# Depthwise convolution accumulated in PSUM four rows at a time, with a frequency stage on single PSUM banks

## The chip, the cores and the metric

One core of one Trainium2 chip runs the whole program. The metric is the device time in microseconds, taken as the median of the runs. An execution's engines are named as in the profile: PE is TensorE's matmuls and PEld its weight loads, DVE is VectorE, ACT is ScalarE, POOL is GpSimd, SP issues the DMAs. SBUF is the on-chip working memory; PSUM is the small memory that matmuls write, eight banks of 512 float32 per partition.

## The reference

Eight images of 128 x 128 pixels and 64 channels, float32, go through two layers.

```python
# layer 0: criss-cross attention
Q, K, V = x @ w_q + b_q, x @ w_k + b_k, x @ w_v + b_v
att = softmax(concat(energies along H (diagonal masked), energies along W))
x = gamma * (att_H applied to V + att_W applied to V) + x
# layer 1: frequency mixing, then a convolutional MLP
h  = layernorm(x) @ w_te + b_te                       # 64 -> 128 channels
F  = fft2(h)                                          # over H and W
fc = gelu(concat(real(F), imag(F)) @ w_fc + b_fc)     # 256 -> 256
sp = real(ifft2(fc[..., :128] + 1j * fc[..., 128:]))
x1 = x + sp @ w_tp + b_tp                             # 128 -> 64
h2 = layernorm(x1) @ w_fe + b_fe                      # 64 -> 128
d  = gelu(depthwise 3x3 convolution of h2 + b_dw)     # 128 channels, SAME padding
out = x1 + d @ w_fp + b_fp                            # 128 -> 64
```

## The kernel before

The program has two parts, one after the other. `attention` runs all eight images in an order written out by hand, and writes its result to DRAM. `mixer` does layer 1; its instructions are ordered by a scheduler, which takes the order of the program as priority and places an instruction when its inputs and buffers are free by its own reckoning. Every engine then works through its own queue in that fixed order. The change is inside `mixer`.

**The frequency stage**, `fourier(b)`, yields after every piece of work, so that other work can be put between. It has three stages. In the W stage, 64 matmuls (L558, tile `aps`) apply the Fourier transform along W, eight channels into one PSUM tile of two banks; ScalarE copies each tile into `at` (L559). In the K stage there are 17 groups of up to four frequencies. A group's transform along H goes through `fps` (L571, L577, L580) and is copied to `f` (L582). One group later, four matmuls of 128 x 512 (`fcps`, L595) apply the 256 x 256 weights: for each half of the output channels, one matmul with `wplus` and one with `wminus`, into the two banks of one PSUM tile. One gelu on ScalarE (L601) empties both banks into `gl`, and GpSimd adds or subtracts the two (L602). One group later still, `gps` (L622; L612 to L616 in the last group, which holds the mean) applies the projection to 64 channels, and ScalarE copies it to `gt` (L625). In the I stage, `inverse_h` transforms back along H (`yps`, L649 to L657), and `inverse_w` transforms back along W (`dps`, L663, two matmuls of 512 into a tile of two banks) while VectorE adds the result to the residual (L669).

**The convolution**, `mlp(b)`, works through an image in 16 chunks of eight rows, with the 128 hidden channels on the partitions. `statistics` (L688) computes the layernorm's deviations on VectorE; `normed` (L694, GpSimd), `transposed` (L703, TensorE) and `expand` (L724, TensorE; L729, ScalarE) make a chunk's hidden rows `h2`. `taps` then accumulates the nine taps of the 3x3 filter for eight rows (1024 elements per partition) in the SBUF tile `acc`: tap 0 on ScalarE with the bias (L746), taps 1 to 8 on VectorE, one `scalar_tensor_tensor` each (L748), which reads `h2` and `acc` and writes `acc`. `gelu` runs on ScalarE in place (L755). `shrink` (L765 on GpSimd, L770 on TensorE) computes the output projection of eight rows, and `store` (L774) adds the residual on VectorE and issues the DMA to DRAM.

**What sets the order.** The driver at the end of `mixer` runs `fourier(b)` and, between its pieces, `mlp(b-1)`: a step of the frequency stage has a weight (`W_STEP`, `K_STEP`, `I_STEP`), and the convolution's 89 pieces are dealt out in proportion. So the first image's frequency stage runs without a convolution, and the last image's convolution without a frequency stage. `load_norm(b+1)` (L542) is put into the I stage.

**PSUM.** The eight banks of `mixer` belong to three pools: `ps_f` (tag `fc`: `aps`, `fcps`, `dps`), two tiles of two banks; `ps_m` (tag `mm`: `fps`, `gps`, `yps`), two of one bank; `ps_c` (tag `mc`: `tpn`, `hp`, `op`), two of one bank. All eight are taken.

Of the kernel before, what the change touches and what calls it, by code (L numbers as in the profile page):

```python
# [21 lines left out]
F32 = mybir.dt.float32  # L22
BF16 = mybir.dt.bfloat16
AF = mybir.ActivationFunctionType
ALU = mybir.AluOpType
# [12 lines left out]
W_STEP, K_STEP, I_STEP = 2.0, 7.0, 5.0  # L38
# [396 lines left out]
def mixer(tc, nc, x2, scale1, tbl, prm, out):  # L435
# [3 lines left out]
    with ExitStack() as ctx:  # L439
# [3 lines left out]
        ps_c = ctx.enter_context(tc.tile_pool(name="m_psc", bufs=2, space=PSUM))  # L443

# [106 lines left out]
        def fourier(b):  # L551
# [3 lines left out]
            for c0 in range(0, C, 8):  # L555
                aps = ps_f.tile([P, 8, P], F32, tag="fc", name="aps")
                for c in range(8):
                    nc.tensor.matmul(aps[:, c, :], lhsT=xn[:, c0 + c, :], rhs=fwd, start=True, stop=True)  # L558
                nc.scalar.copy(at[:, :, c0 : c0 + 8], aps.rearrange("p c k -> p k c"))  # L559
                yield W_STEP  # L560
            gt = big.tile([P, C, 2, 64], F32, tag="big", name="gt")
            pend_fc, pend_tp = None, None
            for g in groups + [None, None]:
# [21 lines left out]
                if pend_fc is not None:  # L585
                    gg, f = pend_fc
                    n = len(gg) * P
                    fv = f.rearrange("p k h -> p (k h)")[:, 0:n]
                    gs = []
                    for half in range(2):  # L590
                        ps = ps_f.tile([P, 2, 512], F32, tag="fc", name="fcps")
                        cols = slice(half * HID, half * HID + HID)
                        for sgn, w in enumerate((wplus, wminus)):
                            mean = gg[0] == 0
                            nc.tensor.matmul(ps[:, sgn, 0:n], lhsT=w[:, cols], rhs=fv, start=True, stop=not mean)  # L595
                            if mean:
                                nc.tensor.matmul(
                                    ps[:, sgn, 0:1], lhsT=dc[:, cols], rhs=ident[0:1, 0:1], start=False, stop=True
                                )
                        gl = p2.tile([P, 2, 512], F32, tag="gl%d" % half, name="gl")  # L600
                        nc.scalar.activation(gl[:, :, 0:n], ps[:, :, 0:n], AF.Gelu, bias=bfc[:, half : half + 1])  # L601
                        nc.gpsimd.tensor_tensor(  # L602
                            gl[:, 0, 0:n], gl[:, 0, 0:n], gl[:, 1, 0:n], ALU.add if half == 0 else ALU.subtract
                        )
                        gs.append(gl)
                    tp_next = (gg, gs)
# [53 lines left out]
        def inverse_w(xs, c0, ys):  # L660
            dps = ps_f.tile([P, 8, P], F32, tag="fc", name="dps")
            for g in range(2):
                nc.tensor.matmul(  # L663
                    dps[:, 4 * g : 4 * g + 4, :].rearrange("p c h -> p (c h)"), lhsT=idw,
                    rhs=ys[:, 4 * g : 4 * g + 4, :].rearrange("p c h -> p (c h)"), start=True, stop=True,
                )
            for s in range(2):
                xv = xs[s][:, :, c0 : c0 + 8]
                nc.vector.tensor_tensor(xv, dps[:, :, 64 * s : 64 * s + 64].rearrange("p c h -> p h c"), xv, ALU.add)  # L669
# [8 lines left out]
        def mlp(b):  # L678
# [4 lines left out]
            xts, h2s, accs = {}, {}, {}  # L683
# [50 lines left out]
            def span(k):  # L734

                return (1 if k == 0 else 0), (CH + 1 if k == n_ch - 1 else CH)

            def taps(k, lo, hi):
                i0, i1 = span(k)
                if lo == 0:  # L740
                    accs[k] = p2.tile([P, CH + 1, P], F32, tag="acc", name="acc")
                av = accs[k][:, 0 : i1 - i0, :]
                for t in range(lo, hi):
                    src = h2s[k][:, i0 + t // 3 : i1 + t // 3, t % 3 : t % 3 + P]
                    if t == 0:
                        nc.scalar.activation(av, src, AF.Identity, bias=bdw, scale=wdw[:, 0:1])  # L746
                    else:
                        nc.vector.scalar_tensor_tensor(  # L748
                            out=av, in0=src, scalar=wdw[:, t : t + 1], in1=av, op0=ALU.mult, op1=ALU.add
                        )  # L750

            def gelu(k):
                i0, i1 = span(k)
                av = accs[k][:, 0 : i1 - i0, :]
                nc.scalar.activation(av, av, AF.Gelu)  # L755

            def shrink(k, a):
# [11 lines left out]
                for i in range(n):  # L769
                    nc.tensor.matmul(op[:, i, :], lhsT=accs[k][:, a + i, :], rhs=wfp, start=True, stop=True)  # L770
# [15 lines left out]
            taps(0, 0, 1)  # L786
            for k in range(n_ch):
                if k > 0:
                    gelu(k - 1)
# [4 lines left out]
                taps(k, 1, 3)  # L794
                yield
                held = shrink(k - 1, 0) if k > 0 else None
                taps(k, 3, 5)
# [3 lines left out]
                taps(k, 5, 6)  # L801
# [5 lines left out]
                taps(k, 6, 8)  # L807
                yield
                if k + 1 < n_ch:
                    taps(k + 1, 0, 1)  # L810
                taps(k, 8, 9)
                yield
            gelu(n_ch - 1)
# [7 lines left out]
        work = W_STEP * 8 + K_STEP * (len(groups) + 2) + I_STEP * 9  # L821
# [65 lines left out]
```

## Time and profile before

| | |
|---|---|
| time, median of 3 | 3831.16 us (3825.0 to 3836.74) |
| span of the profiled execution | 3833.7 us |
| PE busy | 3370.7 us (88%) |
| DVE busy | 2676.3 us (70%) |
| ACT busy | 1741.7 us (45%) |
| POOL busy | 1607.0 us (42%) |
| attention (0 to 1363 us): PE / DVE busy | 1200.6 / 761.3 us |
| mixer (1363 to 3834 us, 2471 us): PE / DVE / ACT / POOL busy | 2170.1 / 1915.0 / 1161.0 / 1127.0 us |
| DMA | 242.94 MB, mean 63 GB/s |

How to read it. A row of the slices has one digit per fortieth of the span (96 us): the tenths of that time in which the engine was busy. A row of a window has its start and end, its length, then the busy time (and number of instructions) of PE, PEld, DVE, ACT and POOL, the granted share of TensorE's clock, the DMA share and GB/s. A row of a group has the line, the engine, the operation, what it writes and reads by the program's tile names and shapes, how often; then its busy time in all and the mean of one in ns; then the idle time of that engine just before it and what ended most of it. A row of the timeline has a start, a duration, and the merged instructions. A row of the waits says which engine and line waited for which, for how long in all, how often, and the longest. A float32 matmul is executed as two passes, so the trace counts it twice. The ends of matmuls are modelled, so a busy TensorE need not be one at its full rate.

### The profile page before, as it was taken

What the parts mean: (1) busy time and instruction counts of PE and PEld (TensorE: products, weight loads), DVE (VectorE), ACT (ScalarE), POOL (GpSimd) and SP (SyncE); (2) the same over time, 40 slices, a digit from 0 to 9 for tenths busy, and PEclk for the clock granted to TensorE, in tenths of its full rate; (3) what the DMA queues carried; (4) which work ended last, traced back from release to release, by engine and by line L of the source; (5) the groups of instructions that cost most, each with busy time, mean ns of one, the idle gap of its engine ahead of it and who ended that gap; (6) DMA issues with size and microseconds to landing.
All of it is one profiled execution on the core that took longest, in us unless ns stands there. A gap on an engine that the chain in (4) does not pass through costs nothing.

```text
span 3833.7 us, 79138 instructions
## 1 busy us (share of the span) xinstructions
PE 3370.7 (88%) x33046; PEld 2387.3 (62%) x33046; DVE 2676.3 (70%) x4432; ACT 1741.7 (45%) x2341; POOL 1607.0 (42%) x1347
## 2 busy tenths in 40 slices
PE   7989989899998679998998998998998998999454
PEld 4666666666666457666665666666665665666333
DVE  3556565664665500788888987888988988978867
ACT  3544535435353233453553553553553554554222
POOL 0333243332433534356356356356356356253111
PEclk7989889999897889998998998998998998999555
DMA  4534434354342511012112112112112112100000
GB/s 101 128 94 121 109 98 124 93 129 108 91 119 69 170 44 45 6 39 58 37 39 58 37 39 58 37 39 58 37 39 58 37 39 53 37 17 17 12 19 20
DMA packets 505190, 242.94 MB, mean 63 GB/s; under 512 B 417026, under 2 KB 486018, under 8 KB 502786
## 3 DMA queue, kind: packets, MB, share of 16 engines
q1 hardware_dynamic: 504834, 237.90, 23.1%
q8 instruction: 260, 4.26, 0.5%
q14 instruction: 96, 0.79, 0.1%
HBM read 169.13 MB, written 67.63 MB: 62 GB/s over the span
## 4 chain that ended last, share of the span: by engine, by line
PE 52%; DVE 26%; issue 8%; POOL 6%; ACT 4%; DMA 2%; SPq 1%; DVEq 0%; POOLq 0%; ACTq 0%
DVE acc L748 18%; PE e L202 6%; PE op L770 5%; PE fcps L595 5%; PE hp L724 4%; PE zp L265 3%; PE yps L655 3%; PE dps L663 3%; PE yps L649 3%; PE sp L289 3%; PE pq L183 3%; PE zp L278 3%; POOL xn L542 2%; PE gps L622 2%; DVE negH L211 2%
## 5 line engine op out<-in xcount | busy, mean ns | idle before, releaser
L748 DVE SCALAR_TENSOR_TENSOR acc<-h,wdw,acc 128x1024 f32<-128x1024 f32 (+2 forms) x1024 | 1612.1, 1594 | 151.5 <-ACT acc L746 131.2
L602 POOL TENSOR_TENSOR gl<-gl 128x512 f32<-128x512 f32 (+2 forms) x272 | 487.1, 1796 | 454.0 <-ACT gl L601 453.9
L770 PE MATMUL op<-wfp,acc 128*128 128x64 f32 x2048 | 292.0, 304 | 163.7 <-ACT acc L755 162.8
L770 PEld LDWEIGHTS op<-wfp,acc 128*128 128x128 f32 x2048 | 278.2, 218 | 187.9 <-ACT acc L755 180.0
L601 ACT ACTIVATE gl<-fcps,bfc 128x1024 f32<-128x1024 f32 (+2 forms) x272 | 292.5, 1077 | 190.7 <-PE fcps L595 180.9
L765 POOL TENSOR_TENSOR ot<-x,bfp 128x512 f32<-128x512 f32 (+1 forms) x144 | 226.2, 1576 | 358.9 <-DMA out_dram<-ot 321.8
L243 ACT ACTIVATE att<-e 128x1024 f32<-128x1024 f32 x256 | 248.3, 1022 | 242.9 <-PE e L202 242.8
L339 POOL TENSOR_TENSOR yo<-yo,xb 128x512 f32<-128x512 f32 x128 | 161.0, 1280 | 430.4 <-issue 296.3
L245 POOL TENSOR_SCALAR_AFFINE_SELECT att<-att 128x1024 f32<-128x1024 f32 x128 | 136.8, 1093 | 419.6 <-ACT att L243 419.6
L729 ACT ACTIVATE h<-hp,bfe 128x512 f32<-128x512 f32 x256 | 171.4, 688 | 291.3 <-PE hp L724 291.1
L595 PE MATMUL fcps<-f,wplus 128*128 128x512 f32 (+2 forms) x544 | 293.7, 622 | 0.0
L622 PEld LDWEIGHTS gps<-wtp,gl 128*128 128x128 f32 x2016 | 246.0, 193 | 57.7 <-issue 55.2
L595 PE MATMUL fcps<-f,wminus 128*128 128x512 f32 (+2 forms) x544 | 275.9, 589 | 0.0
L669 DVE TENSOR_TENSOR x<-dps,x 128x512 f32<-128x512 f32 x128 | 86.2, 683 | 265.2 <-PE dps L663 265.2
L542 POOL TENSOR_TENSOR xn<-xl,scale 128x512 f32<-128x512 f32 x128 | 238.4, 1873 | 57.1 <-DMA xl<-x 56.9
L724 PE MATMUL hp<-xtn,wfe 64*128 64x512 f32 x512 | 243.6, 739 | 21.1 <-DVE ot L774 19.8
L755 ACT ACTIVATE acc<-acc 128x1024 f32<-128x1024 f32 (+2 forms) x128 | 135.4, 1058 | 258.6 <-DVE acc L748 258.6
L202 PE MATMUL e<-qkH 8*128 8x128 f32 (+1 forms) x4096 | 199.7, 316 | 54.4 <-DVE negH L211 50.3
L694 POOL TENSOR_TENSOR xc<-x,scale 128x512 f32<-128x512 f32 x128 | 189.1, 1482 | 129.2 <-PE tpn L703 88.2
L622 PE MATMUL gps<-wtp,gl 128*128 128x64 f32 x2016 | 241.1, 273 | 0.9 <-POOL gl L602 0.9
L202 PEld LDWEIGHTS e<-qkH 8*128 8x128 f32 (+1 forms) x4096 | 164.3, 212 | 122.1 <-DVE negH L211 60.0
L202 PEld LDWEIGHTS e<-qkW 8*128 8x128 f32 (+1 forms) x4096 | 140.6, 194 | 126.4 <-DVE negW L211 36.0
(138 smaller groups left out, 6389.1 us busy)
## 6 DMA issues: line engine op xcount, KB each, us to landing
xl<-in_x_dram SPq DMA_DIRECT2D x256, 128.0 KB
xh<-in_x_dram SPq DMA_DIRECT2D x64, 512.0 KB
xw<-in_x_dram SPq DMA_DIRECT2D x256, 128.0 KB
x<-yo SPq DMA_DIRECT2D x256, 128.0 KB
xl<-x SPq DMA_DIRECT2D x128, 256.0 KB
x<-x SPq DMA_DIRECT2D x16, 2048.0 KB
out_dram<-ot SPq DMA_DIRECT2D x120, 256.0 KB
qkH<-joint SPq DMA_DIRECT2D x256, 2.0 KB
```

The costliest lines, as they stand in the source:

```text
L202: nc.tensor.matmul(es[q // 2][:, q % 2, i, :], lhsT=qk[part, lhs, 4 * (r % 2) + i, :], rhs=qk[part, rhs, 4 * (r % 2) + i, :], start=True, ...
L243: nc.scalar.activation(att, e.rearrange("p q i w -> p (q i) w"), AF.Exp)
L542: nc.gpsimd.tensor_tensor(xn[:, :, h : h + NORM_ROWS], xl.rearrange("p h c -> p c h"), scale1[:, b, h : h + NORM_ROWS].unsqueeze(1).to_bro ...
L595: nc.tensor.matmul(ps[:, sgn, 0:n], lhsT=w[:, cols], rhs=fv, start=True, stop=not mean)
L601: nc.scalar.activation(gl[:, :, 0:n], ps[:, :, 0:n], AF.Gelu, bias=bfc[:, half : half + 1])
L602: nc.gpsimd.tensor_tensor(gl[:, 0, 0:n], gl[:, 0, 0:n], gl[:, 1, 0:n], ALU.add if half == 0 else ALU.subtract)
L622: nc.tensor.matmul(gps[:, j, t, :], lhsT=src[:, 0, j * P : j * P + P], rhs=wtp, start=True, stop=True)
L694: nc.gpsimd.tensor_tensor(xc, rows, scale[:, k * CH : k * CH + CH].unsqueeze(2).to_broadcast([P, CH, C]), ALU.mult)
L724: nc.tensor.matmul(hps[s].rearrange("p j w -> p (j w)"), lhsT=wfe[half, :], rhs=xt[half, :, :].rearrange("p j w -> p (j w)"), start=True, ...
L748: nc.vector.scalar_tensor_tensor(out=av, in0=src, scalar=wdw[:, t : t + 1], in1=av, op0=ALU.mult, op1=ALU.add)
L765: nc.gpsimd.tensor_tensor(ot[:, o : o + m, :], rows, bfp.unsqueeze(1).to_broadcast([P, m, C]), ALU.add)
L770: nc.tensor.matmul(op[:, i, :], lhsT=accs[k][:, a + i, :], rhs=wfp, start=True, stop=True)
```

## The change

Four things go together.

1. The convolution's accumulator moves from SBUF to a new PSUM pool, `ps_a`, of two single banks. A bank holds four rows of 128 pixels, so a chunk's eight rows become two half-chunks (the first chunk has 3 + 4 rows, the last 4 + 4 + 1). Each half has its own chain of nine taps and its own gelu, which reads PSUM and writes a new SBUF tile `gd`, from which the output matmuls read. A tap on VectorE then has one input in SBUF (`h2`) and one in PSUM, and writes PSUM.
2. To free two banks, `ps_f` holds two tiles of one bank in place of two tiles of two. The W stage works in fours of channels instead of eights.
3. In the K stage each of the four matmuls of a group has a bank and a gelu of its own: 512 elements per gelu in place of 1024.
4. In the I stage each of the two matmuls of `inverse_w` has its own bank and its own two adds, of 256 elements in place of 512.

The order in which `mlp` writes out its pieces is drawn up anew for half-chunks, and the W stage's step weight is halved as its steps are doubled. The arithmetic is the same.

```diff
--- before.py
+++ after.py
@@ -35,7 +35,7 @@
 CH = 8
 NORM_ROWS = 8
 
-W_STEP, K_STEP, I_STEP = 2.0, 7.0, 5.0
+W_STEP, K_STEP, I_STEP = 1.0, 7.0, 5.0
 PIECES = 5
 LEAD = 6
 
@@ -441,6 +441,7 @@
         ps_f = ctx.enter_context(tc.tile_pool(name="m_psf", bufs=2, space=PSUM))
         ps_m = ctx.enter_context(tc.tile_pool(name="m_psm", bufs=2, space=PSUM))
         ps_c = ctx.enter_context(tc.tile_pool(name="m_psc", bufs=2, space=PSUM))
+        ps_a = ctx.enter_context(tc.tile_pool(name="m_psa", bufs=2, space=PSUM))
 
         ident = const.tile([P, P], F32, tag="ident", name="m_ident")
         make_identity(nc, ident)
@@ -552,11 +553,11 @@
             im = images[b]
             xn = im["xn"]
             at = big.tile([P, P, C], F32, tag="big", name="at")
-            for c0 in range(0, C, 8):
-                aps = ps_f.tile([P, 8, P], F32, tag="fc", name="aps")
-                for c in range(8):
+            for c0 in range(0, C, 4):
+                aps = ps_f.tile([P, 4, P], F32, tag="fc", name="aps")
+                for c in range(4):
                     nc.tensor.matmul(aps[:, c, :], lhsT=xn[:, c0 + c, :], rhs=fwd, start=True, stop=True)
-                nc.scalar.copy(at[:, :, c0 : c0 + 8], aps.rearrange("p c k -> p k c"))
+                nc.scalar.copy(at[:, :, c0 : c0 + 4], aps.rearrange("p c k -> p k c"))
                 yield W_STEP
             gt = big.tile([P, C, 2, 64], F32, tag="big", name="gt")
             pend_fc, pend_tp = None, None
@@ -588,17 +589,17 @@
                     fv = f.rearrange("p k h -> p (k h)")[:, 0:n]
                     gs = []
                     for half in range(2):
-                        ps = ps_f.tile([P, 2, 512], F32, tag="fc", name="fcps")
+                        gl = p2.tile([P, 2, 512], F32, tag="gl%d" % half, name="gl")
                         cols = slice(half * HID, half * HID + HID)
                         for sgn, w in enumerate((wplus, wminus)):
+                            ps = ps_f.tile([P, 512], F32, tag="fc", name="fcps")
                             mean = gg[0] == 0
-                            nc.tensor.matmul(ps[:, sgn, 0:n], lhsT=w[:, cols], rhs=fv, start=True, stop=not mean)
+                            nc.tensor.matmul(ps[:, 0:n], lhsT=w[:, cols], rhs=fv, start=True, stop=not mean)
                             if mean:
                                 nc.tensor.matmul(
-                                    ps[:, sgn, 0:1], lhsT=dc[:, cols], rhs=ident[0:1, 0:1], start=False, stop=True
+                                    ps[:, 0:1], lhsT=dc[:, cols], rhs=ident[0:1, 0:1], start=False, stop=True
                                 )
-                        gl = p2.tile([P, 2, 512], F32, tag="gl%d" % half, name="gl")
-                        nc.scalar.activation(gl[:, :, 0:n], ps[:, :, 0:n], AF.Gelu, bias=bfc[:, half : half + 1])
+                            nc.scalar.activation(gl[:, sgn, 0:n], ps[:, 0:n], AF.Gelu, bias=bfc[:, half : half + 1])
                         nc.gpsimd.tensor_tensor(
                             gl[:, 0, 0:n], gl[:, 0, 0:n], gl[:, 1, 0:n], ALU.add if half == 0 else ALU.subtract
                         )
@@ -658,15 +659,15 @@
             return ys
 
         def inverse_w(xs, c0, ys):
-            dps = ps_f.tile([P, 8, P], F32, tag="fc", name="dps")
             for g in range(2):
+                dps = ps_f.tile([P, 4, P], F32, tag="fc", name="dps")
                 nc.tensor.matmul(
-                    dps[:, 4 * g : 4 * g + 4, :].rearrange("p c h -> p (c h)"), lhsT=idw,
+                    dps.rearrange("p c h -> p (c h)"), lhsT=idw,
                     rhs=ys[:, 4 * g : 4 * g + 4, :].rearrange("p c h -> p (c h)"), start=True, stop=True,
                 )
-            for s in range(2):
-                xv = xs[s][:, :, c0 : c0 + 8]
-                nc.vector.tensor_tensor(xv, dps[:, :, 64 * s : 64 * s + 64].rearrange("p c h -> p h c"), xv, ALU.add)
+                for s in range(2):
+                    xv = xs[s][:, :, c0 + 4 * g : c0 + 4 * g + 4]
+                    nc.vector.tensor_tensor(xv, dps[:, :, 64 * s : 64 * s + 64].rearrange("p c h -> p h c"), xv, ALU.add)
 
         def lines(xs, lo, hi):
 
@@ -680,7 +681,7 @@
             xs = images.pop(b)["x1"]
             n_ch = P // CH
             scale = p2.tile([P, P], F32, tag="scale2", name="scale2")
-            xts, h2s, accs = {}, {}, {}
+            xts, h2s, accs, gls = {}, {}, {}, {}
 
             def statistics(s):
                 stats = p2.tile([P, 64, 6], F32, tag="stats", name="stats", bufs=1)
@@ -735,11 +736,16 @@
 
                 return (1 if k == 0 else 0), (CH + 1 if k == n_ch - 1 else CH)
 
-            def taps(k, lo, hi):
+            def part(k, u):
+
                 i0, i1 = span(k)
+                return max(i0, 4 * u), min(i1, 4 * u + 4)
+
+            def taps(k, u, lo, hi):
+                i0, i1 = part(k, u)
                 if lo == 0:
-                    accs[k] = p2.tile([P, CH + 1, P], F32, tag="acc", name="acc")
-                av = accs[k][:, 0 : i1 - i0, :]
+                    accs[k, u] = ps_a.tile([P, 4, P], F32, tag="acc", name="acc")
+                av = accs[k, u][:, 0 : i1 - i0, :]
                 for t in range(lo, hi):
                     src = h2s[k][:, i0 + t // 3 : i1 + t // 3, t % 3 : t % 3 + P]
                     if t == 0:
@@ -749,10 +755,11 @@
                             out=av, in0=src, scalar=wdw[:, t : t + 1], in1=av, op0=ALU.mult, op1=ALU.add
                         )
 
-            def gelu(k):
-                i0, i1 = span(k)
-                av = accs[k][:, 0 : i1 - i0, :]
-                nc.scalar.activation(av, av, AF.Gelu)
+            def gelu(k, u):
+                i0, i1 = part(k, u)
+                if u == 0:
+                    gls[k] = p2.tile([P, CH + 1, P], F32, tag="gd", name="gd")
+                nc.scalar.activation(gls[k][:, i0 : i1, :], accs.pop((k, u))[:, 0 : i1 - i0, :], AF.Gelu)
 
             def shrink(k, a):
 
@@ -767,7 +774,7 @@
                     )
                 op = ps_c.tile([P, CH, C], F32, tag="mc", name="op")
                 for i in range(n):
-                    nc.tensor.matmul(op[:, i, :], lhsT=accs[k][:, a + i, :], rhs=wfp, start=True, stop=True)
+                    nc.tensor.matmul(op[:, i, :], lhsT=gls[k][:, i0 + a + i, :], rhs=wfp, start=True, stop=True)
                 return r0, n, ot, op
 
             def store(r0, n, ot, op):
@@ -783,34 +790,39 @@
             yield
             expand(0)
             yield
-            taps(0, 0, 1)
+            taps(0, 0, 0, 1)
             for k in range(n_ch):
                 if k > 0:
-                    gelu(k - 1)
+                    gelu(k - 1, 1)
+                taps(k, 1, 0, 1)
                 if k + 1 < n_ch:
                     transposed(k + 1)
                 if k == 4:
                     statistics(1)
-                taps(k, 1, 3)
+                taps(k, 0, 1, 4)
                 yield
                 held = shrink(k - 1, 0) if k > 0 else None
-                taps(k, 3, 5)
+                taps(k, 0, 4, 8)
                 yield
                 if held:
                     store(*held)
-                taps(k, 5, 6)
+                taps(k, 0, 8, 9)
+                gelu(k, 0)
+                taps(k, 1, 1, 3)
                 yield
                 if k + 1 < n_ch:
                     expand(k + 1)
                 if k + 2 < n_ch:
                     normed(k + 2)
-                taps(k, 6, 8)
+                taps(k, 1, 3, 6)
                 yield
                 if k + 1 < n_ch:
-                    taps(k + 1, 0, 1)
-                taps(k, 8, 9)
+                    taps(k + 1, 0, 0, 1)
+                taps(k, 1, 6, 9)
                 yield
-            gelu(n_ch - 1)
+            gelu(n_ch - 1, 1)
+            taps(n_ch - 1, 2, 0, 9)
+            gelu(n_ch - 1, 2)
             for a in (0, CH):
                 store(*shrink(n_ch - 1, a))
             yield
@@ -818,7 +830,7 @@
 
 
         pieces = LEAD + 3 + PIECES * (P // CH)
-        work = W_STEP * 8 + K_STEP * (len(groups) + 2) + I_STEP * 9
+        work = W_STEP * 16 + K_STEP * (len(groups) + 2) + I_STEP * 9
         for _ in load_norm(0):
             pass
         for b in range(NB + 1):
```

## The prediction

> **What bounds the kernel now.** I read first the page's slices of the span, then windows cut at the stages, then the groups by shape, the waits of one period, and last the timeline around single instructions.
>
> ```profile
> PE   7989989899998679998998998998998998999454
> DVE  3556565664665500788888987888988988978867
> 1363.00:1552.00 189.00, 186.63 (x1336) 137.59 (x1337) 9.02 (x14) 74.67 (x93) 65.93 (x51) 0.98 0.09 26
> 2128.00:2417.00 289.00, 266.09 (x1721) 189.10 (x1720) 245.63 (x299) 145.05 (x193) 151.77 (x118) 0.94 0.16 44
> 3587.00:3834.00 247.00, 115.34 (x376) 80.78 (x376) 175.59 (x150) 70.87 (x95) 36.34 (x58) 0.50 0.08 17
> ```
>
> Attention (0 to 1363 us) is not touched. From there the kernel has three regimes. At 1363 to 1552 the first image's frequency stage runs alone: TensorE (first busy figure) 187 of 189 us, so it is TensorE's. Then come six periods of about 290 us (one is 2128 to 2417), each the frequency stage of image b beside the convolution of image b-1, and a last such stretch of 272 us (3288 to 3560). From 3587 the last convolution runs alone, 247 us, with TensorE at half its clock (0.50).
>
> A period has two nearly full engines, TensorE 266 us and VectorE 246 of 289. TensorE's floor comes from the trace: adding the gaps over 150 ns between matmul starts beyond the streaming time leaves 186 us of work in the lone stage and 259 in a period, so the convolution adds 73, and about 31 us of a period are TensorE waiting. Two thirds of it is ahead of convolution matmuls (L770, L724, L703) and of the mean's matmuls (L612, L613).
>
> ```profile
> L748 DVE SCALAR_TENSOR_TENSOR acc<-h,wdw,acc 128x1024 f32<-128x1024 f32 x896 | 1442.9, 1630 | 129.9 <-ACT acc L746 110.1
> L602 POOL TENSOR_TENSOR gl<-gl 128x512 f32<-128x512 f32 x240 | 435.6, 1820 | 444.7 <-ACT gl L601 444.5
> 2104.68 0.68 DVE L669 TENSOR_TENSOR x<-dps,x 128x512 f32<-128x512 f32 x1
> 2105.28 1.27 DVE L748 SCALAR_TENSOR_TENSOR acc<-h,wdw,acc 128x1024 f32<-128x1024 f32 x1
> 2106.47 0.68 DVE L669 TENSOR_TENSOR x<-dps,x 128x512 f32<-128x512 f32 x1
> ...
> 2206.84 2.59 DVE L748 SCALAR_TENSOR_TENSOR acc<-h,wdw,acc 128x1024 f32<-128x1024 f32 x2
> ...
> 2208.15 3.61 DVE L748 SCALAR_TENSOR_TENSOR acc<-h,wdw,acc 128x1024 f32<-128x1024 f32 x2
> ...
> 2212.97 2.30 POOL L602 TENSOR_TENSOR gl<-gl 128x512 f32<-128x512 f32 x1 [2.30 <-ACT gl L601]
> 2215.32 2.17 POOL L602 TENSOR_TENSOR gl<-gl 128x512 f32<-128x512 f32 x1
> ```
>
> The taps (L748) are two thirds of VectorE's work in a period. One tap of 1024 alone lasts 1.27 us and gives way to the next independent instruction after 1.19 (2105.28 to 2106.47). A tap directly behind the tap it depends on starts 1.31 later (two in 2.59). Beside a GpSimd tensor_tensor it lasts 2.2 to 2.3 (the pair in 3.61), and the GpSimd instruction takes 2.2 to 2.3 instead of about 1.27. Of the 1024 taps 552 overlap one and average 1.86 us; the other 472 average 1.28. That is 552 x 0.58 = 320 us of VectorE time lost to the overlap, and about as much of GpSimd's.
>
> ```profile
> ACT acc L755 <- DVE acc L748: 18.9, 8, 7.2
> DVE acc L748 <- ACT acc L746: 17.6, 6, 4.1
> DVE ot L774 <- PE op L770: 16.5, 5, 7.4
> PEld op L770 <- ACT acc L755: 7.3, 7, 5.1
> ```
>
> These waits of one period (1837 to 2128: total, times, longest) go round one ring: taps, gelu (L755), output matmul (L770), store add (L774), and the first tap on ScalarE (L746).
>
> **What the Trainium skill says.** "SBUF — State Buffer", section Who interferes with whom: a VectorE instruction with two SBUF inputs contends with a GpSimd instruction that reads SBUF, and one with at most one SBUF input does not. The trace agrees on the first half (1.28 against 2.2); L669, with one input in PSUM, is never stretched (mean 683 ns). "Perfetto Trace Analysis", section Optimizing Scalar/DVE Operations: VectorE's overhead per instruction is about 60 ns on SBUF and about 125 on PSUM. The trace shows less for a PSUM input: L669 of 512 elements gives way after 0.60, 0.07 over its 0.53 of elements; a PSUM output is shown nowhere. "TensorE: Matmul & The Clock Gate", section Part 1, says that an idle TensorE window of some 3.4 us halves the clock: the lone convolution does run at 0.50.
>
> **The change, part by part.**
>
> *Taps into PSUM.* 1024 taps become 2112: 1984 of 512 elements, 64 of 384, 64 of 128. From 1024 to 1152 elements an undisturbed tap grows from 1274 to 1407 ns, 1.04 ns per element, so 512 elements stream in 0.53. The slot adds 0.13 (1.19 - 1.07) to an independent tap and 0.25 (1.31 - 1.07) to one behind its own predecessor. The compiled order puts only 317 taps directly behind their predecessor (440 of 1024 before): the two half-chunks alternate. So 317 x 0.78 + 1795 x 0.66 = 1432, less 34 for the small ones: 1398 us. Bounds: L669's overhead (0.60) gives 1271; 65 ns more each, the page's difference of PSUM and SBUF, gives 1535. I take the middle: the trace's PSUM inputs are no dearer, PSUM outputs are unknown. Now: 1024 x 1.594 = 1632, less 0.08 each by which the next starts early, 1552. VectorE saves 154 us (17 to 281), 19 per image.
>
> *GpSimd* no longer meets the taps: L602 falls from 1.8 to about 1.27. It is not full (152 of 289), but its sum stands between gelu and the next matmuls (L612, L622), some 5 us of TensorE's waits.
>
> *Inverse-W adds.* 128 of 0.60 become 256 of 0.34: +9 us in all.
>
> *ScalarE.* The gelu of the frequency stage: 272 x 1.077 becomes 544 x 0.684 (the row of 512): +80. First taps: 0.81 for 512 (1242 ns at 1024, 0.85 per element less): 205 for 159, +45. Convolution gelu: 264 of 0.63 for 128 of 1.06, +28. Copies of `at`: +10. Sum 163 us, 20 per period: ScalarE goes from 145 to 165 of 289, room enough by itself.
>
> *Single banks.* A matmul of 128x512 takes 0.86 (both passes). Bank one is free 0.86 + 0.1 + 0.68 = 1.65 after the start, and the third matmul wants it at 1.72: it just fits if ScalarE comes at once. Where ScalarE is inside another instruction, TensorE waits and everything behind it in its queue with it: two such places in each of 17 groups, ScalarE about two thirds busy there, half an instruction (0.35): up to 8 us per period. The order places output and expand matmuls in between, so I take 4. In the lone first stage ScalarE is idle: +2 in all. `at` in fours: four matmuls take 0.86, the copy 0.58, hidden. The finer step count moves nothing by itself.
>
> *Period.* 290 less half of TensorE's 31 us of waiting, as the ring's VectorE link shortens by 18 of 246 and loses its jitter, plus 4: 279. Seven stretches: -77.
>
> *Last convolution.* Now two chunks of eight rows take 30.8 us, 15.4 each: L774 waits 6.67 and 1.07 in the queue, with taps stuck behind it. After: 16 taps, 13 x 0.66 + 3 x 0.78 = 10.9, the store add 0.60, and 0.7 of wait (gelu 0.63, half the output matmuls at half clock 1.7, handovers 0.35, less three taps placed ahead, 2.0): 12.2. Sixteen chunks: -51; I take -40 for waits not seen.
>
> Sum: -77 + 2 - 40 = -115: 3831 - 115 = 3716.
>
> **The rivals.** (a) *TensorE's floor is reached*: periods of 265, tail -50: 3831 - 7 x 25 - 50 = 3606. For it: TensorE has 259 us of work. Against: the ring and the in-order queues stay, and ScalarE gets more to do. (b) *The gain is eaten by ScalarE*: TensorE waits 8 or more for banks while a gelu waits for taps; periods stay at 290, only the tail gains 35: 3796. For it: ScalarE's queue stops 19 us per period for taps already. (c) *Slower*: taps cost the upper price, 0.72 and 0.85, so VectorE gains nothing that counts, and with 20 us more on ScalarE and single banks the periods grow by 10; tail -20: 3831 + 70 - 20 = 3881. For it: no instruction of the trace writes PSUM from VectorE. Against: PSUM inputs come cheap, and the overlap with GpSimd ends in any case.
>
> **How the numbers follow.** Forecast 0.60 (3716), (a) 0.12, (b) 0.15, (c) 0.13. The range reaches from halfway to (a), 3630, to just past no change, 3838: it holds the forecast and (b) and leaves out most of (a) and (c). Faster by over 0.3% (below 3820) takes the forecast, (a) and most of (b): 0.83; within 0.3% 0.05; slower 0.12.
>
> **What would show it.** Right: taps of 512 lasting 0.70 to 0.80 wherever GpSimd works; L602 near 1.27; a period of 270 to 285 with TensorE's granted clock nearer 1; two chunks of the tail in 24 to 26 us. Wrong: taps over 0.85 (the PSUM price), or matmuls of `fcps` waiting for `gl` over 10 us per period (the banks).

## The result and the profile after

The changed kernel takes 3777.27 us (median of 4 runs, 3772.59 to 3780.67), the kernel before beside it 3828.08 us: ratio 0.987, 95% interval 0.9837 to 0.9904. That is 51 us gained where 115 were forecast. The direction is right and the time lies in the range, but less than half of the gain came.

Cut at the same stages as in the prediction (starts from the first `aps` matmul of each image, the tail from the last `dps` matmul), the two profiled executions give, in us:

| stage | before | after | forecast of the change | change |
|---|---|---|---|---|
| attention, the same instructions | 1363.8 | 1357.8 | 0 | -6.0 |
| lone first frequency stage | 188.3 | 194.8 | +2 | +6.5 |
| six periods | 1736.2 | 1692.8 | -66 | -43.4 |
| last stretch with both | 272.0 | 288.7 | -11 | +16.7 |
| last convolution alone | 273.5 | 243.9 | -40 | -29.6 |

Over all kernels below, the attention part, which nobody touched, took between 1337 and 1364 us, with 264 to 302 us of its first 1330 at a lower granted clock. So a stage of one execution is known to some 2% at best, and what is called faster or slower rests on the timed runs.

The slices of the changed kernel's page, and then its stage windows, to hold against those of before:

```profile
PE   7989999899998769999999999999999999899665
DVE  3566575665755500676877877877877776876888
```

```profile
1357.00:1552.00 195.00, 192.70 (x1336) 137.60 (x1336) 10.89 (x29) 84.70 (x135) 65.88 (x51) 0.98 0.09 25
2107.00:2387.00 280.00, 268.49 (x1725) 182.82 (x1723) 215.45 (x453) 158.80 (x269) 104.85 (x119) 0.99 0.16 46
3533.00:3776.00 243.00, 142.12 (x404) 86.87 (x404) 218.30 (x446) 82.03 (x137) 39.88 (x66) 0.51 0.08 19
```

TensorE's row is now nines, with one eight, until the last convolution. The granted clock of the period shown is 0.99 (0.94 before), that of all six periods 0.97 (0.93 before), and that of the last stretch 0.94 (0.97 before). VectorE fell from 246 to 215 us of a period and GpSimd from 152 to 105, both by as much as forecast or more. But TensorE, with the same matmuls in its program, is busy for 268.5 us of a period of 280, where it was busy for 266.1 of 289. It waits less, and it has more to do.

The taps, GpSimd's sums and the output side, by shape:

```profile
L754 DVE SCALAR_TENSOR_TENSOR acc<-h,wdw,acc 128x512 f32<-128x512 f32 x1984 | 1383.4, 749 | 192.8 <-ACT acc L752 179.4
L603 POOL TENSOR_TENSOR gl<-gl 128x512 f32<-128x512 f32 x240 | 304.6, 1269 | 531.8 <-ACT gl L602 510.8 <-issue 20.9
L725 PE MATMUL hp<-xtn,wfe 64*128 64x512 f32 x512 | 295.1, 711 | 1.5 <-ACT xtn L708 1.4 <-ACT h L730 0.2
```

And around single instructions (VectorE, one stretch with the residual adds between the taps, one without):

```profile
2099.70 0.75 DVE L754 SCALAR_TENSOR_TENSOR acc<-h,wdw,acc 128x512 f32<-128x512 f32 x1
2100.36 0.42 DVE L670 TENSOR_TENSOR x<-dps,x 128x256 f32<-128x256 f32 x1
2100.69 0.75 DVE L754 SCALAR_TENSOR_TENSOR acc<-h,wdw,acc 128x512 f32<-128x512 f32 x1
...
2189.85 5.63 DVE L754 SCALAR_TENSOR_TENSOR acc<-h,wdw,acc 128x512 f32<-128x512 f32 x8
```

A tap into PSUM gives way after 0.66 us (2099.70 to 2100.36), an add of 256 after 0.33, and eight taps take 5.63, 0.70 each, with GpSimd at work or not: the 954 taps of 512 that overlap a GpSimd tensor_tensor last 0.75 us on average, and so do those that overlap nothing of GpSimd's. The sum takes 1.27 us in place of 1.82. The price of PSUM that rival (c) feared does not exist here.

The third row holds the surprise. `hp`, the two matmuls of `expand`, are 512 records in both kernels, but cover 295 us of TensorE instead of 244. Here are the group before, one chunk's `hp` with both matmuls together and one matmul that stands alone (before), and then two of the changed kernel's (TensorE; a float32 matmul is two passes, so x4 is both matmuls and x2 is one):

```profile
L724 PE MATMUL hp<-xtn,wfe 64*128 64x512 f32 x512 | 243.6, 739 | 21.1 <-DVE ot L774 19.8 <-ACT xtn L707 1.4
2193.23 1.13 PE L724 MATMUL hp<-xtn,wfe 64*128 64x512 f32 x4
...
2206.97 1.12 PE L724 MATMUL hp<-xtn,wfe 64*128 64x512 f32 x2 [0.42 <-DVE ot L774]
```

```profile
2182.24 1.12 PE L725 MATMUL hp<-xtn,wfe 64*128 64x512 f32 x2
2183.29 1.12 PE L597 MATMUL fcps<-f,wminus 128*128 128x512 f32 x2
...
2186.10 1.12 PE L725 MATMUL hp<-xtn,wfe 64*128 64x512 f32 x2
2187.15 1.12 PE L597 MATMUL fcps<-f,wminus 128*128 128x512 f32 x2
```

Together, both matmuls last 1.13 us. Alone, each lasts 1.12, and the next matmul starts 1.05 behind it: where the two don't stand side by side in TensorE's order, the second costs as much again. Each uses 64 of the 128 input partitions, that is, one half of the array's rows. Over the whole program 79 of 128 such pairs were adjacent before and 22 after. In a period it is 9 of 16 before and 2 after (8 in the first period).

### The profile page after: what moved, and what is told of

Read it like the earlier page. It is cut to its first block, busy times and chain, and to the rows that moved or that the text cites. A ratio compares the mean times of both kernels' runs of the same rounds, so it can differ in the third digit from the quotient of the medians.

```text
span 3778.0 us, 81178 instructions
## 1 busy us (share of the span) xinstructions
PE 3435.8 (91%) x33046; PEld 2376.6 (63%) x33046; DVE 2485.9 (66%) x5648; ACT 1854.7 (49%) x2949; POOL 1294.5 (34%) x1347
## 4 chain that ended last, share of the span: by engine, by line
PE 56%; DVE 8%; issue 3%; ACT 3%; POOL 3%; DMA 2%; SPq 0%; POOLq 0%; DVEq 0%; ACTq 0%
PE fcps L597 12%; PE op L777 6%; DVE acc L754 6%; PE hp L725 6%; PE gps L623 5%; PE aps L559 4%; PE yps L650 4%; PE fps L572 3%; PE fps L578 3%; PE yps L656 3%; PE dps L664 2%; PE tpn L704 2%; PE e L202 1%; POOL xn L543 1%; DMA xl<-x 1%
## 5 line engine op out<-in xcount | busy, mean ns | idle before, releaser
L754 DVE SCALAR_TENSOR_TENSOR acc<-h,wdw,acc 128x512 f32<-128x512 f32 (+2 forms) x2112 | 1430.4, 733 | 207.0 <-ACT acc L752 193.2
L603 POOL TENSOR_TENSOR gl<-gl 128x512 f32<-128x512 f32 (+2 forms) x272 | 332.5, 1223 | 543.1 <-ACT gl L602 522.2
L602 ACT ACTIVATE gl<-fcps,bfc 128x512 f32<-128x512 f32 (+2 forms) x544 | 360.6, 670 | 168.6 <-PE fcps L597 128.9
L777 PEld LDWEIGHTS op<-wfp,gd 128*128 128x128 f32 x2048 | 288.6, 214 | 207.0 <-ACT gd L762 159.9
L777 PE MATMUL op<-wfp,gd 128*128 128x64 f32 x2048 | 308.5, 300 | 111.2 <-ACT gd L762 111.1
L725 PE MATMUL hp<-xtn,wfe 64*128 64x512 f32 x512 | 295.1, 711 | 1.5 <-ACT xtn L708 1.4
L597 PE MATMUL fcps<-f,wplus 128*128 128x512 f32 (+2 forms) x544 | 293.2, 621 | 0.5 <-ACT gl L602 0.5
L781 DVE TENSOR_TENSOR ot<-op,ot 128x512 f32<-128x512 f32 (+2 forms) x136 | 89.5, 659 | 292.5 <-PE op L777 276.1
L772 POOL TENSOR_TENSOR ot<-x,bfp 128x512 f32<-128x512 f32 (+1 forms) x144 | 167.3, 1165 | 300.8 <-DMA out_dram<-ot 261.0
L670 DVE TENSOR_TENSOR x<-dps,x 128x256 f32<-128x256 f32 x256 | 104.8, 417 | 237.5 <-PE dps L664 236.5
L762 ACT ACTIVATE gd<-acc 128x512 f32<-128x512 f32 (+2 forms) x264 | 154.8, 587 | 216.1 <-DVE acc L754 215.8
L695 POOL TENSOR_TENSOR xc<-x,scale 128x512 f32<-128x512 f32 x128 | 133.3, 1044 | 321.0 <-PE tpn L704 216.8
```

What stands on the lines that cost most here:

```text
L597: nc.tensor.matmul(ps[:, 0:n], lhsT=w[:, cols], rhs=fv, start=True, stop=not mean)
L602: nc.scalar.activation(gl[:, sgn, 0:n], ps[:, 0:n], AF.Gelu, bias=bfc[:, half : half + 1])
L603: nc.gpsimd.tensor_tensor(gl[:, 0, 0:n], gl[:, 0, 0:n], gl[:, 1, 0:n], ALU.add if half == 0 else ALU.subtract)
L725: nc.tensor.matmul(hps[s].rearrange("p j w -> p (j w)"), lhsT=wfe[half, :], rhs=xt[half, :, :].rearrange("p j w -> p (j w)"), start=True, ...
L754: nc.vector.scalar_tensor_tensor(out=av, in0=src, scalar=wdw[:, t : t + 1], in1=av, op0=ALU.mult, op1=ALU.add)
L772: nc.gpsimd.tensor_tensor(ot[:, o : o + m, :], rows, bfp.unsqueeze(1).to_broadcast([P, m, C]), ALU.add)
```

## The experiments

The first four ran on one chip (the kernel before there: 3831.95 us), the next four on another (3824.17), the last three in a third group (3823.56). So ratios to the kernel before are what is compared between groups.

Theory A: what is missing from the gain was lost in TensorE's own stream, because `op` now fills its bank in two portions (the gelus come in halves), holds one of the two `mc` banks longer, and so drives the two `hp` apart. Theory B: single banks and the finer ScalarE instructions ate it. Theory C: taps into PSUM are dear.

### hp in a pair of banks of its own

In the changed kernel, and with the same edit in the kernel before:

```diff
-  hps = [ps_c.tile([P, 4, P], F32, tag="mc", name="hp") for _ in range(2)]
+  hpt = ps_c.tile([P, 2, 4, P], F32, tag="hp", name="hp", bufs=1)
+  hps = [hpt[:, s, :, :] for s in range(2)]
...
-  tp = ps_c.tile([P, 4, P], F32, tag="mc", name="tpn")
+  tp = ps_m.tile([P, 4, P], F32, tag="mm", name="tpn")
...
-  op = ps_c.tile([P, CH, C], F32, tag="mc", name="op")
+  op = ps_m.tile([P, CH, C], F32, tag="mm", name="op")
```

> The changed kernel with the two PSUM banks of expand's two matmuls (hp) in one tile of a pool of their own, so that the two stand next to each other on TensorE (115 of 128 in the compiled order instead of 22); tpn and op move to the frequency stage's two banks to make room. Theory A (the missing gain is TensorE time: two adjacent hp matmuls run on two halves of the array at once and take 1.06 us together, apart 1.05 each): 93 pairs x 1.05 = 98 us less TensorE work, part of it lost to tpn and op waiting for shared banks, so 3690 to 3730. Theory B (the missing gain went to the single banks, where matmuls of fcps wait for the gelu): 3770 to 3790, since their banks are as before.

Measured 3627.67 us, ratio 0.9473 (0.9443 to 0.9503). That is 150 us below the changed kernel and more than A expected.

> The same move of hp, tpn and op in the kernel before, nothing else: 128 of 128 hp pairs adjacent instead of 79. Theory A: 49 pairs x 1.05 = 51 us of TensorE work less, of which VectorE's contended taps may hide half: 3780 to 3805. Theory B: no change, 3820 to 3835.

Measured 3782.73 us, ratio 0.9888 (0.9861 to 0.9915), as expected, but not where A would have it. All 16 pairs of a period are adjacent (9 before), worth 7 x 1.05 = 7.4 us, and the period shrank by 2.4. In the profiled executions the gain lies in the last convolution (273.5 to 241.2), where all 16 pairs were adjacent before, and in the attention part. In the kernel before, most of what TensorE saves in a period is lost again: by the measure of the table further down, its work falls by 9.7 us a period, its waiting grows by 3.6, and 3.7 more are lost to the lower clock. Pairs pay in full only in periods with fewer waits.

### The half-chunks in SBUF

The changed kernel with the accumulator back in SBUF, halves and all:

```diff
-  accs[k, u] = ps_a.tile([P, 4, P], F32, tag="acc", name="acc")
+  accs[k, u] = p2.tile([P, 4, P], F32, tag="acc", name="acc", bufs=4)
```

There are four buffers in place of two banks, the gelu works in place, and `op` reads the half it needs. So the run takes the placement together with these.

> The changed kernel with its half-chunk accumulators back in SBUF (four half-chunk buffers, gelu in place), single banks kept: what the placement in PSUM alone is worth. If taking the taps off the port shared with GpSimd is what brings the gain: taps that overlap a GpSimd sum go from 0.75 to 1.3 us and more, GpSimd's sums back to 1.8, and the time to 3830 to 3880. If TensorE's stream is all that counts now (53 hp pairs adjacent here, 31 more than in the changed kernel): 3740 to 3790.

Measured 3921.82 us, ratio 1.0229 (1.0195 to 1.0264): slower than the kernel before, 145 us slower than the same with PSUM, and above what was expected of the contention alone. The rows of this kernel that stand against the first two groups above:

```profile
L753 DVE SCALAR_TENSOR_TENSOR acc<-h,wdw,acc 128x512 f32<-128x512 f32 x1984 | 1794.6, 960 | 103.5 <-ACT acc L751 100.3
L602 POOL TENSOR_TENSOR gl<-gl 128x512 f32<-128x512 f32 x240 | 393.9, 1642 | 464.1 <-ACT gl L601 463.9
```

A tap of 512 takes 960 ns on average in SBUF and 749 in PSUM, GpSimd's sum 1642 against 1269. The overlap makes the difference: in SBUF the 764 taps that overlap a GpSimd tensor_tensor average 1.31 us and those that overlap nothing 0.74, in PSUM both average 0.75. `hp` can't be the reason, as this kernel has more adjacent pairs than the changed one (53 for 22). Theory C is dead, with the sign reversed.

### Single banks

The kernel before with the single-bank edits of the frequency stage alone (points 2 to 4 of the change), the convolution untouched:

> The kernel before with the frequency stage on single banks and nothing else (convolution as before, hp pairs as before, two banks left unused): the price of the single banks alone. Theory A: the lone first stage gains 6 us as in the changed kernel, the periods 1 to 3 us each: 3840 to 3858. Theory B: 64 us or nearly: 3870 to 3900.

Measured 3889.97 us, ratio 1.016 (1.0131 to 1.0188): +58 us, as B expected and twice what the prediction put in. The adjacent pairs are the same 79, so this is a cost apart from A's. A weight load of `fcps` now waits for the gelu that frees its bank; TensorE also waits longer for GpSimd's sums in the last group (L612, L613; one period of this kernel: for whom, total, times, longest):

```profile
PEld fcps L596 <- ACT gl L601: 16.7, 25, 3.1
...
PEld gps L613 <- POOL gl L602: 5.4, 1, 5.4
PE gps L613 <- POOL gl L602: 5.2, 1, 5.2
```

Three runs took it apart: `fcps` alone, `aps` and `dps` alone, and all three with as many banks as before, the last by

```diff
-  ps_f = ctx.enter_context(tc.tile_pool(name="m_psf", bufs=2, space=PSUM))
+  ps_f = ctx.enter_context(tc.tile_pool(name="m_psf", bufs=4, space=PSUM))
```

> The kernel before with one of the three single-bank edits alone: fcps in single banks with a gelu for each, while aps and dps stay in pairs of banks. Taps, half-chunks and expand are as before (79 adjacent hp pairs in both). All three edits together cost 58 us (3890). If the bank that a matmul of fcps must wait for is the price, nearly all of it is here: 3870 to 3890 us. If it lies in the finer aps and dps steps, 3830 to 3845.

Measured 3872.00 us, ratio 1.0117 (1.0095 to 1.0139).

> The kernel before with the other two single-bank edits alone: aps and dps in single banks, fcps in pairs of banks. If the price of single banks is that of fcps, 3825 to 3845 us; if it lies here, 3860 to 3890.

Measured 3850.55 us, ratio 1.0062 (1.0042 to 1.0082), a little above what was expected of it if the price were that of `fcps`. So the first of these edits is about two thirds of the price and the other two a third.

> The kernel before with all three single-bank edits, as in the run of 3890 us, but with four single banks for them in place of two, so that the frequency stage has as much PSUM as before. Theory A (a matmul of fcps waits for the gelu that frees its bank): with twice the banks the gelus have another 1.7 us to come, and most of the 58 us goes away: 3825 to 3855 us. Rival (the price is ScalarE's: 272 more gelu instructions and 80 more us of it, which delay GpSimd's sums and the matmuls behind them): it stays at 3870 to 3890 us.

Measured 3856.71 us, ratio 1.0087 (1.0061 to 1.0113). Both theories got half. With four banks the lone stage is back at 187.6 us (188.3 before, 197.4 with two), and the waits of the weight loads for `gl` are gone:

```profile
PEld fcps L596 <- ACT gl L601: 0.9, 2, 0.8
...
PEld gps L613 <- POOL gl L602: 5.3, 1, 5.3
...
PEld gps L612 <- POOL gl L602: 4.5, 1, 4.5
```

So about 0.7% (28 us) of the 1.6% is the wait for a bank, and 0.9% (33 us) is left of finer instructions with no shortage of banks; the intervals of the two ratios leave this division uncertain by some 0.4%. In its trace the last group's matmuls wait 9.8 us for GpSimd's sums, 4.9 before, which is about what its periods are longer by (293.2 us for 289.4). What makes the finer `aps` and `dps` steps cost time is not known.

### Is it the overlap in the array, or the order and the banks?

The weights of `hp` padded with zeros to all 128 input partitions, so that each matmul fills the array and two can't lie side by side; order and banks unchanged. Once in the paired kernel and once in the changed kernel:

```diff
-  half = slice(64 * s, 64 * s + 64)
...
-  ... lhsT=wfe[half, :], rhs=xt[half, :, :] ...
+  ... lhsT=wfz[:, s, :], rhs=xt ...
```

> The kernel with paired hp (3628 us), with one thing changed: the weights of expand's two matmuls are held twice, padded with zeros to all 128 input partitions, so that each matmul takes the whole array. The order of TensorE's stream and the banks are the same (114 adjacent pairs); the zeros change nothing in what is computed. Theory A (two adjacent matmuls on 64 input partitions each run side by side, and that is what the pairs are worth): a pair goes from 1.06 us to two of about 0.86, +0.66 x 114 = +75, the single ones fall by 0.19 x 28 = -5, so +70 on an engine that is at work for 250 of the 263 us of a period: 3680 to 3705 us. Rival (what was worth the time was the order and the banks, not the overlap in the array): 3615 to 3640 us.

Measured 3674.31 us, ratio 0.9617 (0.9588 to 0.9647) against 0.9473: slower by 1.4% of the kernel before. One pair of it, with the matmul that follows:

```profile
2142.65 1.94 PE L728 MATMUL hp<-xtn,wfz 128*128 128x512 f32 x4
2144.42 0.60 PE L707 MATMUL tpn<-m_ident,xc 128*128 128x128 f32 x4
```

A pair now takes 1.77 us to the start of the next matmul, 1.06 with half the rows each. From start to start `hp` takes 30.2 us of a period against 18.9, and the period grew by 7.5.

> The changed kernel (3777 us), with the same padded weights and nothing else: 22 adjacent pairs and 212 single hp matmuls, as in it. Theory A: a single hp of 64 input partitions takes 1.05 us, one of the whole array about 0.86, so 212 x -0.19 = -40, and the 22 pairs +0.66 x 22 = +15, together -25: 3740 to 3760 us, that is, the padding that slows the paired kernel speeds this one. Rival (the length of hp is not on the path, waits set the period): 3770 to 3785 us.

Measured 3713.03 us, ratio 0.9716 (0.9686 to 0.9746) against 0.987: the same edit makes this kernel faster by 1.5%. A single `hp` fell from 1.05 us to 0.91. Both signs are as A says, and nothing else proposed here gives the padding opposite signs. (The padded kernels also hold `scale2` in one buffer, to make room; that is the same in both.) The gain is 59 us (1.5% of 3824) where A had 25, and in part that is because A left out the matmul ahead. `hp` itself takes 2.8 us less of a period (32.5 to 29.7). But a matmul that fills the array also gives way later when a half-array `hp` comes next: a pass of `gps` after 205 ns in place of 112, one of `fcps` of 512 after 523 in place of 429. Ahead of a padded `hp` these 0.09 us are gone, and there are 30 such places in a period (28 lone `hp`, 2 pairs). In the seven stretches with both layers' work (the six periods and the last one) TensorE's work falls by 39 us and the stretches by 54; the rest of these 54 is less waiting and less time at half clock. Another 9 us lie in the attention part of the profiled executions, which the edit doesn't touch.

### op on another bank

One line in the changed kernel:

```diff
-  op = ps_c.tile([P, CH, C], F32, tag="mc", name="op")
+  op = ps_m.tile([P, CH, C], F32, tag="mm", name="op")
```

> The changed kernel with one word changed: op takes its bank from the pool of gps, fps and yps in place of the pool that hp and tpn share. hp stays two tiles of one bank. In the compiled order 104 pairs are adjacent, against 22 in the changed kernel and 114 with the two-bank tile. Theory A (op holding a bank of hp's is what splits the pairs): 82 more pairs x 1.05 us = -86, so 3680 to 3700 us; more gain than that (down to 3640) would say that op's hold on the bank also costs waits. Rival (the two-bank tile or tpn's move brought the gain of the paired kernel): 3750 to 3780 us.

Measured 3624.91 us, ratio 0.9487 (0.9457 to 0.9517). The whole gain of the paired kernel is in this line; the two-bank tile and the move of `tpn` add nothing that these runs can tell. A period of it, `hp` over the program, and two passes of `yps`:

```profile
2054.00:2317.00 263.00, 251.37 (x1722) 177.34 (x1723) 214.78 (x453) 157.88 (x269) 104.55 (x119) 0.99 0.17 49
```

```profile
L725 PE MATMUL hp<-xtn,wfe 64*128 64x512 f32 x512 | 188.4, 711 | 18.1 <-ACT xtn L708 18.1
2246.89 0.32 PE L656 MATMUL yps<-tb,gt 128*64 128x128 f32 x1
2246.90 0.32 PE L657 MATMUL yps<-tb,gt 128*64 128x128 f32 x1
```

VectorE, ScalarE, GpSimd and the clock are as in the changed kernel's period (214.78, 157.88, 104.55, 0.99). Only TensorE is shorter, 251 for 268 us, and the period with it, 263 for 280. `hp` covers 107 us less of TensorE over the program (188.4 for 295.1), 78 of them in the seven stretches. In the profiled executions these stretches are 137 us shorter: TensorE's work in them falls by 110 us and its time lost to half clock by 31, while its waiting stays. Of the 110, `hp` has 70. Some 34 are in `yps` and `fps`. Those of them with 64 columns of weights run side by side in twos as well, as the last two rows show, and the changed kernel had parted some of these (782 passes of `yps` start beside their partner in it, 882 here and before). Of the rest of the time, 18 us lie in the attention part and 9 in the last convolution.

The trace shows how `op` parts a pair:

```profile
2182.24 1.12 PE L725 MATMUL hp<-xtn,wfe 64*128 64x512 f32 x2
2185.29 0.69 DVE L781 TENSOR_TENSOR ot<-op,ot 128x512 f32<-128x512 f32 x1 [1.91 <-PE op L777]
2186.10 1.12 PE L725 MATMUL hp<-xtn,wfe 64*128 64x512 f32 x2
```

The first `hp` finds one of the two banks free, and `op` holds the other until the store add (L781) has read it. In the changed kernel such an add ends between the two `hp` in 91 of the 92 pairs that are parted in the seven stretches, and the second `hp` starts a median of 0.54 us after its end. With `op` elsewhere that happens in none.

### op in one go

In the changed kernel `op`'s matmuls of the first half are queued behind those of the second, so that the bank is held for a short time; banks as they are:

```diff
-  for i in range(n):
-      nc.tensor.matmul(op[:, i, :], ...)
+  def project(i):
+      return nc.tensor.matmul(op[:, i, :], ...)
...
+  last = project(n - 1)
+  with tc.issue_after(...last...):
+      for i in range(n - 1):
+          project(i)
```

> The changed kernel with op's eight matmuls in one go: those of the first half-chunk are queued behind those of the second, banks as they are. In the compiled order 42 pairs are adjacent, against 22. Theory A with pairs alone: 20 x 1.05 = -21, so 3750 to 3765 us. If op's split filling by itself holds the bank long enough to cost waits beyond the pairs, more: 3700 to 3740. Rival (op's split does nothing): 3770 to 3785.

Measured 3787.45 us, ratio 0.9911 (0.9881 to 0.9941): no gain, a miss. The 42 adjacent pairs are there, and `hp` covers 16 us less (278.9 for 295.1), but in a period only 3 of 16 are adjacent against 2; the rest lie in the last convolution (16 against 2), which isn't TensorE's, and that stage got longer (262 us for 244), as the output matmuls, now all behind the second gelu, end later. A pair is worth its 1.05 us only where TensorE is the bound. In the stretches `op` now holds its bank for a median of 2.7 us, from its first matmul to the end of the store add, in place of 11.1. Yet that add still ends between the two `hp` in 80 of the 86 parted pairs. So it isn't the long hold that parts a pair, and theory A's reason is not borne out; what the runs show is that `op` has a bank of the pair's pool when the first `hp` comes.

## Why the prediction was wrong

Step by step, as it put them:

- *Taps into PSUM*: right. An independent tap was to take 0.66 us and takes 0.66; the sum was to be 1398 us and is 1430 of busy time, overlaps counted once, inside the bounds of 1271 to 1535. The page "Perfetto Trace Analysis" of the Trainium skill, section Optimizing Scalar/DVE Operations, gives VectorE an overhead of about 125 ns on PSUM and 60 on SBUF; that difference is not borne out. Over 0.53 us of elements the slot adds 0.13 in PSUM, as it did for the taps in SBUF, and an undisturbed tap of 512 lasts 0.75 us in PSUM and 0.74 in SBUF.
- *GpSimd*: right, 1.27 us as said (1269 ns).
- *Inverse-W adds*: right, 0.33 each for 0.34.
- *ScalarE*: its size was right (159 us of a period for 165). "Room enough by itself" is in doubt: with the banks given back, the finer instructions of the frequency stage still cost 33 us in the kernel before (ratio 1.0087), though no run shows how much of that is ScalarE's.
- *Single banks*: 4 us a period and 2 in the lone stage, 30 in all, agrees with the 28 that four banks gave back, but the edits as a whole cost 58, and the lone stage grew by 6.5. The sign that the prediction named, over 10 us of `fcps` waiting for `gl` in a period, came: 13.4 in the changed kernel, nearly all at the weight loads.
- *Period*: this is the step that failed. It took TensorE's 259 us of work as a floor that the change doesn't move, and let only the waiting shrink. The floor itself was read too high. Where the trace grants half the clock (0.5), a pass of 128 columns gives way after 213 ns in place of 112, and the prediction's measure counts part of that as work. The table takes that measure (what is over 150 ns beyond the streaming time is waiting), but counts a matmul at full clock and puts what half clock adds to it in a column of its own. Means of the six periods, in us:

| kernel | work | lost to half clock | waiting | length | adjacent hp of 16 |
|---|---|---|---|---|---|
| before | 248.9 | 17.7 | 22.8 | 289.4 | 9 |
| single banks only | 250.2 | 20.7 | 27.0 | 297.9 | 9 |
| after | 263.3 | 7.8 | 11.1 | 282.1 | 2 (first: 8) |
| after, hp padded | 257.7 | 8.2 | 10.0 | 275.9 | 2 (first: 8) |
| after, op elsewhere | 247.6 | 4.4 | 11.6 | 263.7 | 12 (first: 16) |
| after, hp paired | 244.2 | 6.3 | 13.0 | 263.5 | 15 |

Waiting and half clock together fell by 21.6 us a period, more than the 15 - 4 = 11 forecast. But the work grew by 14.4, and the prediction had put nothing there. Over the seven stretches it grew by 100 us: 45 of them in `hp`, which is 43 lost pairs at 1.05; some 20 in `fcps`, most of which the single banks bring by themselves; 19 in `yps`, whose pairs were parted too; 8 in `dps`. The period shown above lasts 279.4 us, just the 279 forecast, and that is luck: two errors cancel in it, and the mean of the six is 282.1.

With `op` elsewhere the period is 264 us, close to the 265 of rival (a), "TensorE's floor is reached". So the convolution's move did bring TensorE near its floor; the change raised the floor at the same time. Rival (b), the gain eaten by ScalarE and banks at unchanged periods, came nearer in time (3796) than the forecast, but its periods did not stay: they shrank by 7 us, and banks are only a part of what ate the gain.

- *The last stretch* failed by 28 us, and is part of the same step: it was counted as a period like the others, though it had only 14 us of waiting and 9 of half clock to give back. Its work grew from 249 to 263 us, and here half clock took more than before, 16 us; with `op` elsewhere the stretch takes 261.7 in place of 288.7.
- *Last convolution*: right in kind. Two chunks take 27.2 us at the rows below and 26.1 later (24 to 26 forecast; 30.8 before), -29.6 of -40. With the halves in SBUF the stretch takes 255.4 us, so some 18 of the 29.6 come without PSUM. The rows show what a chunk's end waits for now: 1.24 us ahead of this store add and 0.45 ahead of later ones, for 6.67 and 1.07 in turn before.

```profile
3606.65 0.69 DVE L781 TENSOR_TENSOR ot<-op,ot 128x512 f32<-128x512 f32 x1 [1.24 <-PE op L777]
3607.26 11.73 DVE L754 SCALAR_TENSOR_TENSOR acc<-h,wdw,acc 128x512 f32<-128x512 f32 x17
```

The steps of the change, in timed medians: single banks +58, halves in SBUF another +32, PSUM for the accumulator -145, and -152 more had `op` been given another bank.

The part of the loss that is `hp`'s could have been read before the run: the compiled order of the changed kernel shows 22 adjacent `hp` pairs for 79, and the trace before shows four passes in 1.13 us where one matmul alone takes 1.12 (at 2206.97 us). The Trainium skill has the fact too: "TensorE: Matmul & The Clock Gate", section Part 3: Packing small matmuls — row/col tiling, says that matmuls in different row tiles run concurrently. The traces agree: 1.06 us for two adjacent, 1.05 for one, 1.77 for two that fill the array.

What stays open: why the `aps` and `dps` edits cost time; what of the 33 us left with four banks is ScalarE's; and what sets the half clock, which took 31 us less of the stretches once `op` had another bank. Freeing banks for the frequency stage inside the kernel with `op` elsewhere wasn't tried.

## What to carry to other kernels

Before an engine's work is taken as a floor, check that the change leaves the order of its stream alone: here two half-array matmuls cost one only as long as nothing came between them, and a third tile in their pool of two was enough to part them. When tiles get finer, ask of each pool who holds a buffer when a pair needs two, and give that tile a pool that no pair depends on; here a shorter hold was no help. A saving on an engine is worth its length only in the stages which that engine bounds; count it stage by stage.

## What the hardware showed that was not expected

VectorE reading and writing PSUM in place cost no more than in SBUF: an undisturbed tap of 512 elements lasted 0.75 us for 0.74. And it took away the contention with GpSimd on both sides, 960 to 749 ns for a tap and 1642 to 1269 for a sum. A matmul on 64 input partitions alone took 1.05 us to the next start, longer than one padded to 128 (0.91), and the full-array pass ahead of it gave way 0.09 us later. The granted clock of the six periods was 0.93 before, 0.97 after and 0.98 with `op` elsewhere, in step with less waiting; that the waits set it is not shown by a run of its own.
